# Image 0's tanh, tokens and features woven into its first layer, chunk by chunk

## The chip, the cores and the metric

The kernel runs on one core of one Trainium2 chip. The metric is the device time of one execution in microseconds (us), from the first to the last instruction of the core with a little around it. The engines are named as the profile names them: PE (TensorE, matrix products), DVE (VectorE), ACT (ScalarE), POOL (GpSimd) and SP (SyncE, which here issues the DMAs).

## What is computed

Eight images of 128 channels and 36x36 positions (1296 tokens) go through two layers. The first normalises in groups, convolves to queries, keys and values, and attends with a softmax; the second treats each position as a token, with an additive attention and a layer of 64 experts. Cut to what matters here:

```python
# layer 0, of the group-normalised x
x = conv1x1(inp, w_x)
q, k, v = conv3x3(x, w_qx), conv3x3_valid(x, w_kx), conv3x3_valid(x, w_vx)
a_x = softmax(q.T @ k) @ v                 # 1296 queries, 34*34 = 1156 keys
h = tanh(w_h[x, a_x, c-part] + b_h)
x = inp + w_o @ h + b_o
# layer 1, on tokens t (1296 x 128 per image)
n = layernorm(t)
s[i, j] = sum_d w[d] * tanh((n Wq)[i, d] + (n Wk)[j, d])   # additive scores
t = t + softmax(s) @ n
t = t + experts(layernorm(t))
```

## The kernel before, in words

The scores of layer 1 take nearly all of the time. The kernel writes the sum of tanh terms as quotients of products of exponentials over 8 blocks of 128 features (`NF = 8`). For one block of queries and one tile of keys a *slot* has four small products on PE, two denominators `d` and two numerators `n` (line 976), Ln and Exp of the denominators on ACT (999 and 1002: the reciprocal), the products of numerators and reciprocals on DVE (1027, 1029, 1033), and sums on POOL (1042). Twelve slots make a unit: one image, one chunk of 432 queries (`CH`, three chunks an image) and one tile of 128 keys (`KT`, eleven tiles, the last with 16 keys; `order` is 0, 1, 2, 3, 4, 10, 5, 6, 7, 8, 9).

All engines run in the order in which the code issues instructions; nothing is reordered. The order around the slots is written out with generators. A function such as `layer0`, `tokens` or `keys` issues a few instructions and yields: `matmuls(n)` asks for a turn on PE after n slots, `step(n)` for a turn without PE, `TAKE` to go on at once. During the slots four lanes hold such generators (`first_of_all`, `urgent`, `gates`, `background`). Every third slot gives a matmul turn; an allowance of 370 columns a slot (`PACE`) limits what a turn issues, except for `first_of_all`. The next image's first layer, tokens and keys run this way in `background` behind the current image's slots. Image 0 has no slots before it, so its preparation runs alone, at the start:

1. `normal(0)` normalises; `signs` lets POOL write a table of signs; `conv_keys(0)` convolves the keys.
2. `layer0(0)` (line 417) convolves the values, projects them (`vw`), and then for each chunk of 432 queries convolves the queries, makes scores and exponentials of ten key tiles, sums them, divides, and writes the chunk's part of `hpre` (line 506). The sums `tot` are made by POOL. Beside it, from its tenth step on, one step each of `context` (a constant part of the bias) and `features` (line 541: the weight products with `sign`, `a_q`, `a_k` and a few columns) is issued for each of its steps. After the third chunk one Tanh over all 1296 columns (line 509), which needs another table of functions than Exp and Ln, and three products with `w_o` whose results are added to x (line 517).
3. `tokens(0)` (line 589) transposes all eleven tiles, writes the tokens to memory (`tokd`), takes mean and variance of each token, raises the variance to the power -1/2 on POOL (line 265), transposes again and normalises into `xh`, and transposes that into `xT`.
4. `keys(0)` for the first tile, and four query blocks (`new_block`, lines 710 and 711), are issued in full; then the first three slots' denominators, and keys of two more tiles. Then the slots start, and the lane `urgent` holds the other keys.

In the slots, `exps` (line 1056) takes the exponential of a unit's scores. At the second one of each chunk it runs `urgent` until nothing is left in it.

`prefetch(u + 2)` loads the keys of the unit after next at the first slot of each unit, so a tile's keys have to be issued by then. Big tiles have eight buffers, chunk tiles (128x432) eight, and PSUM gives four banks to `aux` and the numerators.

Of the kernel before, what the change touches and what calls it, by code (L numbers as in the profile page):

```python
# [3 lines left out]

# [6 lines left out]
F32 = mybir.dt.float32  # L11
AF = mybir.ActivationFunctionType
ALU = mybir.AluOpType
# [59 lines left out]
def kernel(  # L73
# [56 lines left out]
    with ExitStack() as loop, ExitStack() as score:  # L130
# [143 lines left out]
        def step(rest=1):  # L274
            return (False, rest)

        def matmuls(rest=0):
            return (True, rest)
# [3 lines left out]
        def bmm(out, lhsT, rhs, **kw):  # L282
            behind[0] += max(out.free_size(), 128) + 20
            mm(out, lhsT, rhs, **kw)  # L284
# [123 lines left out]
        def conv_keys(b):  # L408
# [3 lines left out]
            for r0, nr in KROWS:  # L412
                yield from conv_turns(
                    taps["k"], (r0, nr), 1, grid(k[:, r0 * WV : (r0 + nr) * WV], WV), True
                )

        def layer0(b):

            r = xs[b][:, :N]
# [31 lines left out]
            for c in range(NCH):  # L451
# [52 lines left out]
                   xpad[:, 1 + c * RC : 1 + (c + 1) * RC, 1 : 1 + W], start=True, stop=True)  # L504
                yield TAKE
                nc.vector.tensor_add(hp[:, cols], px[:, :CH], ax)
                yield matmuls()
            yield step(2)
            nc.scalar.activation(hp, hp, AF.Tanh, bias=hb)
            nc.scalar.preload_act_table_set(LNEXP)  # L510
# [78 lines left out]
        def tokens(b):  # L589
# [74 lines left out]
                nc.sync.dma_start(xr[32 * i : 32 * i + REM], xh[:REM, NKT - 1, :])  # L664
            prepared[b] = (xh, xT, xr)

        def keys(b, tiles):

            xT = prepared[b][1]
            yield matmuls(1)  # L670
            for t in tiles:
# [4 lines left out]
                for q0 in (0, NF // 2):  # L676
                    some = slice(q0, q0 + NF // 2)
                    pk = aux("pk1").rearrange("p (q t) -> p q t", t=128)
                    for q in range(NF // 2):
                        bmm(pk[:, q, :n], a_k[:, (q0 + q) * 128 : (q0 + q + 1) * 128],  # L680
                           xT[:, o : o + n], start=True, stop=True)
                    yield TAKE
                    if first:
# [19 lines left out]
        def query_block(b, c, q, qf):  # L703

            xT = prepared[b][1]
            pq = aux("pq1")
            bmm(pq[:, :CH], a_q[:, q * 128 : (q + 1) * 128], xT[:, c * CH : (c + 1) * CH],
               start=True, stop=True)
            yield TAKE
            nc.scalar.activation(qf[:, 0, :], pq[:, :CH], AF.Exp, bias=fb_s[:, q : q + 1])  # L710
            nc.gpsimd.tensor_scalar(  # L711
                qf[:, 1, :], qf[:, 0, :], cs_s[:, q : q + 1], None, ALU.mult
            )
            yield matmuls()

# [210 lines left out]
        def drain(*gens):  # L926
            for g in gens:
                for _ in g:
                    pass
# [34 lines left out]
        def new_block(b, c, q):  # L964
            qf = qfp.tile([128, 2, CH], F32, tag="qf", name="qf")
            qf_of[b, c, q] = qf
            return query_block(b, c, q, qf)
# [88 lines left out]
        def exps(p, u, d):  # L1056
            b, c, j = units[u]

            while urgent and len(es.get((b, c), ())) == 1:
                urgent.run(p)  # L1060
            e = etp.tile([128, CH], F32, tag="e", name="e")
            nc.scalar.activation(e[:, : d.shape[-1]], d, AF.Exp, bias=eb_s)  # L1062
            es.setdefault((b, c), {})[j] = e
            if (b, c) == (NB - 1, NCH - 1) and len(es[b, c]) == NKT - 2:
                urgent.append(attend_early(b, c, es[b, c]))
            if len(es[b, c]) == NKT:
                urgent.append(attend(b, c, es.pop((b, c))))
# [61 lines left out]
        sign = signs()  # L1129
        drain(conv_keys(0))  # L1130

        aside = chain(context(), features(sign))
        for i, _ in enumerate(layer0(0)):
            if i > 8:
                next(aside, None)
        drain(aside)
        a_q, a_k, cs_s, fb_s, eb_s = (feat[n] for n in ("a_q", "a_k", "cs_s", "fb_s", "eb_s"))
        drain(tokens(0), keys(0, order[:1]))
        for i, q in enumerate(IN_TURN):
            if i < 4:  # L1140
                drain(new_block(0, 0, q))
            else:
                first_of_all.append(new_block(0, 0, q))
        for p in range(LAG):
            denominators(p)
        drain(keys(0, order[1:3]))
        prefetch(1)
        urgent.append(keys(0, order[3:]))
        pending = deque()
        for p, (u, k) in enumerate(slots):  # L1150
            b, c, j = units[u]
# [260 lines left out]
```

## Time and profile before

| | |
|---|---|
| median of 3 runs | 6119.27 us (6111.72 to 6121.77) |
| the profiled execution | 6131.19 us |
| its span, first to last instruction | 6129.5 us |
| PE / DVE / ACT / POOL busy | 92% / 78% / 87% / 75% of the span |
| last add into `hpre` of image 0 (line 506) | starts at 129.16 us |
| first denominator product of a slot | starts at 155.57 us |
| first numerator product of a slot | starts at 162.32 us |
| mean granted clock of TensorE | 0.982 of full speed |

The profile is one execution. A *stretch* view gives the busy time of each engine between two times, with the granted clock of PE as a share of full speed. The *timeline* gives instructions in order of time; in brackets it says how long the engine had been idle and what released it. The *chain of waits* goes back from the end, at each step to what released it. Matrix products in 32-bit floats show as two instructions each.

### The profile page before, as it was taken

What the parts mean: (1) busy time and instruction counts of PE and PEld (TensorE: products, weight loads), DVE (VectorE), ACT (ScalarE), POOL (GpSimd) and SP (SyncE); (2) the same over time, 40 slices, a digit from 0 to 9 for tenths busy, and PEclk for the clock granted to TensorE, in tenths of its full rate; (3) what the DMA queues carried; (4) which work ended last, traced back from release to release, by engine and by line L of the source; (5) the groups of instructions that cost most, each with busy time, mean ns of one, the idle gap of its engine ahead of it and who ended that gap; (6) DMA issues with size and microseconds to landing.
All of it is one profiled execution on the core that took longest, in us unless ns stands there. A gap on an engine that the chain in (4) does not pass through costs nothing.

```text
span 6129.5 us, 94280 instructions
## 1 busy us (share of the span) xinstructions
PE 5669.4 (92%) x33500; PEld 2928.9 (48%) x33500; DVE 4786.5 (78%) x9544; ACT 5338.2 (87%) x5859; POOL 4603.0 (75%) x2824
## 2 busy tenths in 40 slices
PE   7999999999999999999999999999999999988886
PEld 5554455544554445544445444454445544544433
DVE  4787878878788788877787777887778878788883
ACT  1999898998989989889998999899998998999991
POOL 4777777877778867778687786877777777777871
PEclk9999999999999999999999999999999999999998
DMA  1210021001110011100111001110011000110008
GB/s 44 73 34 22 25 74 40 20 25 33 66 39 20 26 46 54 37 24 23 61 39 39 22 24 65 40 33 23 28 62 49 24 25 28 66 50 29 28 20 286
DMA packets 150409, 270.42 MB, mean 44 GB/s; under 512 B 45553, under 2 KB 75633, under 8 KB 149937
## 3 DMA queue, kind: packets, MB, share of 16 engines
q1 hardware_dynamic: 149936, 264.39, 13.0%
q8 instruction: 264, 4.33, 0.3%
q14 instruction: 209, 1.70, 0.1%
HBM read 200.15 MB, written 63.93 MB: 43 GB/s over the span
## 4 chain that ended last, share of the span: by engine, by line
PE 54%; DVE 16%; ACT 15%; issue 11%; POOL 2%; DMA 1%; SPq 0%; DVEq 0%; POOLq 0%; ACTq 0%
PE d L976 18%; PE n L976 12%; ACT lq L999 11%; PE pa L284 7%; DVE rp L1033 7%; PE pc L284 5%; DVE n L1027 5%; PE s L284 3%; DVE accd L1029 2%; PE pq L284 2%; PE pk L284 1%; PE d L981 1%; PE n L981 1%; ACT e L1062 1%; DMA w<-in_weight_dram 1%
## 5 line engine op out<-in xcount | busy, mean ns | idle before, releaser
L1042 POOL TENSOR_TENSOR accp<-accp,rp 128x864 f32<-128x864 f32 x1439 | 2912.2, 2024 | 995.3 <-DVE rp L1033 951.4
L976 PE MATMUL d<-qf,kf 32*128 32x432 f32 (+1 forms) x11520 | 2785.5, 562 | 269.3 <-ACT lq L999 264.0
L976 PE MATMUL n<-qf,kf 32*128 32x432 f32 (+1 forms) x11520 | 2997.9, 556 | 31.0 <-DVE rp L1033 12.4
L999 ACT ACTIVATE lq<-d 128x864 f32<-128x864 f32 x2928 | 2483.2, 877 | 473.9 <-PE n L976 284.6
L1033 DVE TENSOR_TENSOR rp<-n,lq 128x432 f32<-128x432 f32 x3912 | 2180.2, 600 | 757.5 <-PE n L976 606.3
L1002 ACT ACTIVATE lq<-lq 128x864 f32<-128x864 f32 (+1 forms) x1944 | 2495.8, 1284 | 61.7
L976 PEld LDWEIGHTS d<-qf,kf 32*128 32x128 f32 (+1 forms) x11520 | 1024.4, 185 | 1447.4 <-ACT lq L999 1105.5
L976 PEld LDWEIGHTS n<-qf,kf 32*128 32x128 f32 (+1 forms) x11520 | 1263.1, 186 | 700.4 <-issue 294.8
L1029 DVE TENSOR_TENSOR accd<-n,accd 128x432 f32<-128x432 f32 x1440 | 866.1, 601 | 24.6
L1027 DVE TENSOR_TENSOR n<-n,lq 128x432 f32<-128x432 f32 x1440 | 810.3, 607 | 59.1 <-PE n L976 37.1
L1040 POOL TENSOR_TENSOR accp<-rp 128x864 f32<-128x864 f32 x240 | 485.6, 2023 | 286.6 <-DVE rp L1033 284.4
L284 PE MATMUL pa<-xh,e 128*108 128x129 f32 x1920 | 254.9, 281 | 32.7 <-DVE accd L1029 27.7
L284 PEld LDWEIGHTS pa<-xh,e 128*108 128x108 f32 x1920 | 221.0, 174 | 127.4 <-DVE accd L1029 102.6
L1051 POOL TENSOR_TENSOR accd<-accp,accd 128x432 f32<-128x432 f32 x239 | 265.4, 1110 | 18.7
L1049 POOL TENSOR_TENSOR accp<-accp 128x432 f32<-128x432 f32 x239 | 263.9, 1104 | 11.8
L711 POOL TENSOR_SCALAR qf<-qf,cs_s 128x432 f32<-128x432 f32 x192 | 260.3, 1366 | 9.2 <-ACT qf L710 9.2
L462 POOL TENSOR_TENSOR tot<-tot,e 116x432 f32<-116x432 f32 x192 | 212.2, 1105 | 9.0 <-ACT e L471 4.5
L284 PE MATMUL s<-q,k 128*116 128x432 f32 x480 | 207.0, 547 | 7.8 <-DVE accd L1029 5.5
L471 ACT ACTIVATE e<-s 116x432 f32<-116x432 f32 x240 | 116.3, 521 | 99.1 <-PE s L284 97.9
L284 PE MATMUL pa<-e,vw 116*128 116x432 f32 x480 | 196.8, 532 | 0.4
L284 PEld LDWEIGHTS pk<-xT,a_k 128*128 128x128 f32 x1408 | 164.8, 192 | 54.2 <-DVE accd L1029 43.5
L1022 DVE TENSOR_TENSOR accd<-n,lq 128x432 f32<-128x432 f32 x240 | 143.8, 599 | 49.6 <-ACT lq L1002 26.3
(223 smaller groups left out, 3826.5 us busy)
## 6 DMA issues: line engine op xcount, KB each, us to landing
kf<-kd SPq DMA_DIRECT2D x239, 512.0 KB
kd<-ks SPq DMA_DIRECT2D x158, 256.0 KB
w<-in_weight_dram SPq DMA_DIRECT2D x32, 1024.0 KB
wk_t<-wk_t_d SPq DMA_DIRECT2D x7, 768.0 KB
wv_t<-wv_t_d SPq DMA_DIRECT2D x7, 768.0 KB
wq_t<-wq_t_d SPq DMA_DIRECT2D x7, 768.0 KB
x<-in_x_dram SPq DMA_DIRECT2D x8, 648.0 KB
t<-tokd SPq DMA_DIRECT2D x96, 54.0 KB
```

What stands on the lines that cost most here:

```text
L284: mm(out, lhsT, rhs, **kw)
L711: nc.gpsimd.tensor_scalar(qf[:, 1, :], qf[:, 0, :], cs_s[:, q : q + 1], None, ALU.mult)
L976: mm(outs[h][:, :CH], kf[rows[h], q, :], qf_of[b, c, q][rows[h], part, :], start=True, stop=True)
L999: nc.scalar.activation(lq[:, o : o + n, :], d[:, :n, :CH], AF.Ln)
L1002: nc.scalar.activation(some, some, AF.Exp, scale=-1.0)
L1027: mult(ns[h], ns[h], lq[:, o + h, :])
L1029: nc.vector.tensor_add(live["d"], ns[h], live["d"])
L1033: mult(rp[:, h, :], n, lq[:, o + h, :])
L1040: nc.gpsimd.tensor_add(live["p"], live["r"], rp)
L1042: ending(u if k == NP - 1 else 0).tensor_add(live["p"], live["p"], rp)
L1049: ending(u).tensor_add(s[:, 0, :], s[:, 0, :], s[:, 1, :])
L1051: ending(u).tensor_add(d, s[:, 0, :], d)
```

## The change

In image 0 the tanh is no longer one Tanh over three chunks but is made for each chunk with a clamp, Exp, Ln and Exp (1 - 2/(1 + e^2x)), which are all in the table that the kernel uses anyway. `layer0(0)` returns after the last chunk of `hpre`. What followed, for image 0 alone, is a new generator `first_tokens(c, hp)` for each chunk: the tanh in four steps, the product with `w_o`, the sum with x, transposes, token statistics, normalisation and transposes for the tiles that the chunk completes (tiles 0 to 2, 3 to 5, 6 to 10). It transposes the tokens once, not twice, before it normalises.

The steps beside `layer0(0)` start later (after its step 24 instead of 8), and they are now a queue: `context`, `features`, then, when a chunk is done, its `first_tokens`; after chunk 1 also the keys of tile 0 and four query blocks. A step that asks for a rest makes the queue wait for twice as many steps of `layer0`. What is left at the end is issued at once, beside the third chunk's tanh. The rest of `first_tokens(2)` goes into the lane `urgent`, behind the keys of two tiles and ahead of the other keys, and `exps` doesn't empty the lane for the first chunk of image 0.

```diff
+        def tanh_parts(h):
+            def limited():
+                nc.vector.tensor_scalar(h, h, hb, 15.0, ALU.add, ALU.min)
+            def exp():
+                nc.scalar.activation(h, h, AF.Exp, scale=2.0)
+            def log():
+                nc.scalar.activation(h, h, AF.Ln, bias=ones[:, 0:1])
+            def share():
+                nc.scalar.activation(h, h, AF.Exp, scale=-1.0)
+                nc.gpsimd.tensor_scalar(h, h, -2.0, 1.0, ALU.mult, ALU.add)
+            return limited, exp, log, share
...
                 nc.vector.tensor_add(hp[:, cols], px[:, :CH], ax)
+                if b == 0:
+                    first_chunk_done(c, hp)
                 yield matmuls()
+            if b == 0:
+                return
             yield step(2)
...
+        def first_tokens(c, hp):
+            r = xs[0][:, :N]
+            if c == 0:
+                xh = big_tile("xh")[:, : NKT * (C + 1)].rearrange("p (t c) -> p t c", c=C + 1)
+                nc.gpsimd.memset(xh[:, :, C : C + 1], 1.0)
+                xr = two.tile([128, C + 1], F32, tag="xr", name="xr")
+                prepared[0] = (xh, big_tile("xT")[:, :N], xr)
+            xh, xT, xr = prepared[0]
+            cols = slice(c * CH, (c + 1) * CH)
+            for part in tanh_parts(hp[:, cols]):
+                yield step(1)
+                part()
+            yield matmuls(2)
+            po = aux("po0")
+            bmm(po[:, :CH], wo_s, hp[:, cols], start=True, stop=True)
+            yield TAKE
+            nc.vector.scalar_tensor_tensor(
+                r[:, cols], po[:, :CH], bo_s, r[:, cols], ALU.add, ALU.add
+            )
+            yield matmuls(1)
+            for some in ([(0, 1, 2)], [(3, 4, 5)], [(6, 7, 8), (9, 10)])[c]:
+                tp = aux("tpl")
+                for i, t in enumerate(some):
+                    o, n = KT[t]
+                    turned_to(tp[:n, i * C : (i + 1) * C], r[:, o : o + n], ident)
+                yield TAKE
+                tok = chunk_tile("tok")[:, : 3 * C].rearrange("p (t c) -> p t c", c=C)
...
+                nc.vector.tensor_copy(
+                    tok[:, :full, :], tp[:, : full * C].rearrange("p (t c) -> p t c", c=C)
+                )
+                o = KT[some[0]][0]
+                nc.sync.dma_start(
+                    tokd[0][o : o + full * 128].rearrange("(t p) c -> p t c", p=128),
+                    tok[:, :full, :],
+                )
...
+                for i, t in enumerate(some):
+                    n = KT[t][1]
+                    nc.vector.bn_stats(st[:n, i, :], tok[:n, i, :])
+                    nc.vector.bn_aggr(mv[:n, i, :], st[:n, i, :])
+                ve = plus_eps(mv[:, : len(some), 1], 1e-5, [128, len(some)])
+                yield step(1)
+                rs = small.tile([128, 3], F32, tag="ln_rs", name="ln_rs")[:, : len(some)]
+                rsqrt(rs, ve)
+                yield step(2)
+                for i, t in enumerate(some):
+                    n = KT[t][1]
+                    nc.vector.tensor_scalar(
+                        xh[:n, t, :C], tok[:n, i, :], mv[:n, i, 0:1], rs[:n, i : i + 1],
+                        ALU.subtract, ALU.mult,
+                    )
+                yield matmuls(1)
+                tp = aux("tpc")
+                for i, t in enumerate(some):
+                    n = KT[t][1]
+                    turned_to(tp[:, i * 128 : i * 128 + n], xh[:n, t, :C], ident[:n, :n])
+                yield TAKE
+                lo, hi = KT[some[0]][0], KT[some[-1]][0] + KT[some[-1]][1]
+                nc.vector.tensor_copy(xT[:, lo:hi], tp[:, : hi - lo])
+                yield matmuls()
...
-            while urgent and len(es.get((b, c), ())) == 1:
+            while urgent and (b, c) != (0, 0) and len(es.get((b, c), ())) == 1:
                 urgent.run(p)
...
-        aside = chain(context(), features(sign))
+        aside = deque([context(), features(sign)])
+
+        def first_chunk_done(c, hp):
+            if c == NCH - 1:
+                urgent.append(first_tokens(c, hp))
+                return
+            aside.append(first_tokens(c, hp))
+            if c == 1:
+                aside.append(keys(0, order[:1]))
+                aside.extend(new_block(0, 0, q) for q in IN_TURN[:4])
+
+        rest = 0
         for i, _ in enumerate(layer0(0)):
-            if i > 8:
-                next(aside, None)
-        drain(aside)
...
-        drain(tokens(0), keys(0, order[:1]))
-        for i, q in enumerate(IN_TURN):
-            if i < 4:
-                drain(new_block(0, 0, q))
-            else:
-                first_of_all.append(new_block(0, 0, q))
+            if rest > 0 or i <= 24 or not aside:
+                rest -= 1
+                continue
+            says = next(aside[0], 0)
+            if says == 0:
+                aside.popleft()
+            elif says is not None:
+                rest = 2 * says[1]
+        left = list(aside)
+        for i in range(5):
+            next(urgent[0])
+            drain(*left[i : i + 1])
+        drain(*left[5:])
+        first_of_all.extend(new_block(0, 0, q) for q in IN_TURN[4:])
         for p in range(LAG):
             denominators(p)
         drain(keys(0, order[1:3]))
         prefetch(1)
-        urgent.append(keys(0, order[3:]))
+        urgent.appendleft(keys(0, order[3:5]))
+        urgent.append(keys(0, order[5:]))
```

## The prediction

> **What bounds the kernel now.** I read the page first: how full each engine is over the whole span.
>
> ```profile
> PE 5669.4 (92%) x33500; PEld 2928.9 (48%) x33500; DVE 4786.5 (78%) x9544; ACT 5338.2 (87%) x5859; POOL 4603.0 (75%) x2824
> ```
>
> The change touches image 0 only, so the average says little. I then asked for the busy time of each engine in stretches: 30 to 66 us (the values' convolution, the features, the first query convolution), 66 to 129 (the three chunks of image 0's attention), 129 to 162 (from the last chunk to the first slot), and in the slots 196 to 230 (with keys) and 230 to 262 (without).
>
> ```profile
> core 0: us, PE busy (x) PEld busy (x) DVE busy (x) ACT busy (x) POOL busy (x), PEclk, DMA share, GB/s
> 30.00:66.00 36.00, 30.29 (x166) 26.59 (x164) 13.80 (x43) 0.00 (x0) 17.02 (x19) 0.91 0.01 1
> 66.00:129.00 63.00, 58.24 (x180) 32.71 (x180) 16.54 (x33) 20.50 (x37) 29.75 (x28) 1.00 0.00 0
> 129.00:162.00 33.00, 21.81 (x106) 14.75 (x107) 13.79 (x46) 11.66 (x14) 7.61 (x6) 0.79 0.12 38
> 196.00:230.00 34.00, 33.21 (x216) 18.93 (x214) 25.55 (x47) 33.65 (x40) 23.56 (x14) 1.00 0.38 130
> 230.00:262.00 32.00, 25.13 (x152) 12.08 (x154) 30.34 (x58) 31.59 (x34) 25.70 (x17) 1.00 0.10 30
> ```
>
> In 66 to 129 PE is the bound and DVE, ACT and POOL are mostly idle. In 129 to 162 nothing is full: a chain. In the slots ACT is full (31.59 of 32 us), DVE follows (30.34), PE has a fifth to spare without keys. The chain of waits, 112 to 166 us, gives the serial stretch (start, length, engine, work):
>
> ```profile
> 129.16 0.62 DVE hpre L506
> ...
> 129.80 1.38 ACT hpre L509
> ...
> 131.23 4.15 PE po L284 x6
> ...
> 136.07 1.55 DVE tok L608 x3
> ...
> 142.83 2.16 POOL ln_rs L265
> ...
> 147.07 2.61 PE tpc L288 x11
> 149.68 3.06 PE pk L284 x16
> 152.74 2.90 PE pq L284 x8
> 155.64 0.95 PE d L976 x8
> ```
>
> From the last `hpre` to the first `d` 26 us go by, one engine at a time. The timeline of PE has another hole earlier, and the start of the slots' numerators (start, length; in brackets the idle time before and its releaser):
>
> ```profile
> 47.62 2.07 PE L556 MATMUL pa<-sign,wT 128*128 128x512 f32 x2 [5.69 <-POOL sign L532]
> ...
> 66.46 3.16 PE L284 MATMUL s<-q,k 128*116 128x432 f32 x8 [0.48 <-DVE q L316]
> ...
> 162.32 0.60 PE L976 MATMUL n<-qf,kf 32*128 32x432 f32 x1
> ```
>
> The features' matmul waits for the signs that POOL writes until 47.56, with the values' convolution queued behind it on PE.
>
> **What the Trainium skill says.** "ScalarE: Activation LUTs", section "What ACT_TABLE_LOAD costs", gives a load of 1283 ns, and its section "Table sets: the hidden batching unit" says that one set holds Exp and Ln. The trace agrees: loads of 1.28 us stand only around the Tanh (127.42 and 131.19), none between Ln and Exp. "TensorE: Matmul & The Clock Gate", section "What's actually happening", says that PE goes to half clock after an idle window of some 3.4 us. The trace agrees: granted clock 0.51 in 48 to 53 us, just after the wait for the signs, and 0.50 in 145 to 149, in the serial stretch. "Trainium Architecture — The Big Picture", section "Inside one NeuronCore", says that each engine runs its own stream and meets the others only at semaphores: a step woven into another engine's idle time is free, but its wait holds whatever is queued behind it. The hole at 47 us is one.
>
> **The change, part by part.** All sums are against the profiled execution (span 6129.5, its time 6131.19). The unprofiled runs have the median 6119.27, 12 us less; I take the difference over to it unchanged.
>
> (a) *Features later.* The steps beside image 0's layer started at step 9; now they start at step 25, when the values' convolution is issued (steps 1 to 24). The signs are then long done and PE meets no hole. PE's work from 29.9: convolution of v 12 groups, 4 at 1.13 and 8 at 1.04 (the cadence of the keys' convolution just before) = 12.8; projection vw 2.4; context 2.06 + 0.28; two transposes 0.3 each; four sign products of 2 x 0.43, with overheads 3.6; the query convolution 4.5; the products for `cs` 1.9, which now cover the 0.8 us that the first scores waited for q. Sum 28.2 with 1 us of hand-offs 29.2: first scores at 59.1 instead of 66.46. Gain 7.4: the hole of 5.7 and the half clock behind it. The DMA of `wvc_s` has only its place among the steps moved; SP has nothing else queued there.
>
> (b) *Chunk 0's and chunk 1's tokens inside chunks 1 and 2.* Added to each of them: on PE the output product 0.72, three transposes twice, 0.45 + 0.5: 1.7 us, which bounds there, so it counts in full. On DVE the clamp 0.4 (128x384 took 0.36), residual 0.67, and copies, statistics and normalisation 4.1, beside 8 us busy of 22. ACT takes Exp, Ln, Exp of 0.55 each. POOL takes the share 1.37 (the row of `qf`, same shape) and the power over 3 columns, about 1.0 (11 took 2.15, one 0.60 to 0.83); it has 0.65 us to spare per two score tiles, and the chunk's end waits for its total already (PE `pt` 0.92). I take 1.0 more for that and for PE standing at `po`, where the share may be 0.3 late. Cost 2.7 a chunk, 5.4 in all; bounds 3.4 (PE alone) and 12. Their SP writes to `tokd` land under the chunk. The clamp, two Exps and Ln have no row of their own before; same-shape rows stand in. Chunk buffers: `tok` takes one of eight for about 4 us; q, tot and ax hold three, four stay for e, and an e lives about 3.5 us with a new one each 0.7 to 2 us. Just enough; taken as nothing.
>
> (c) *The serial stretch.* Gone: Tanh with its load, the long chain of tokens. First keys (`pk`, x16) and four query blocks stay; the keys now stand around chunk 2's `pt`, at full clock about 2.05 as in the slots. From the start of `pt` (125.24): pt 1, pk 1, pa 1.45, pk 1, px and pq0 1.4: first query Exp on ACT at 131.3. Then ACT is the path: four query Exps 2.8 and, between them, chunk 2's Exp, Ln, Exp 1.7: denominators' Ln at 135.6; Ln and Exp of three slots 5.0: 140.6; the first keys of the next tile 0.6, which free the PSUM buffer of the first numerator: 141.2. Before it was 162.3. Gain 21.1.
>
> (d) *Chunk 2's tokens in the slots.* After four key turns the lane gives `po` at slot 11, then transposes, statistics and normalisation up to about slot 26. ACT takes nothing of it, PE 2.5 us that its spare fifth hides. DVE is what it costs: residual 0.67; first group of three tiles 0.55 + 1.19 + 0.17 + 0.98 + 0.55; second 0.27 + 0.27 + 0.78 + 0.17 + 0.65 + 0.30, memset 0.1: 6.65. Its slack is 0.37 per three slots of 4.97 (4.6 busy), 1.9 over five turns, with half a key more 2.4: 4.3 stick out. POOL's two powers, 1.8, add 0.7. Cost 5; bounds 0 (the DVE work of image 1's normalisation at 247 to 255 stretched nothing) and 12. Keys behind it move from slots 8 to 29 to slots 8 to 47, each at least a unit ahead of its load; image 1's own steps start no later than the lane's rests allow, and they now end at 849 us with 53 us to spare before image 1.
>
> (e) *No emptying at the second exponential of (0,0).* Before, the lane was empty by then (last keys at 223.3, that exponential at 226.25): nothing. It only keeps (d) from a burst.
>
> Sum: -7.4 + 5.4 - 21.1 + 5.0 = -18.1, so 6111.4 for the profiled time's span and **6101** for the median.
>
> **Rivals.** *Less of it arrives* (6111): in-order waits inside chunks 1 and 2 cost 12 instead of 5.4, and the slots 8 instead of 5: -7.4 + 12 - 21.1 + 8 = -8.5 remain. For it: POOL has little slack there, and every step stands on two engines. Against: each step is put three to six steps after what it needs, 1.4 us or more. *The slots absorb everything* (6094): (d) costs nothing and (b) PE alone, -7.4 + 3.4 - 21.1 = -25.1. For it: image 1's normalisation passed unseen. Against: DVE's slack is counted. *Slower* (6137): the tokens' steps starve the slots until PE's clock halves. In image 1's slots, 755 to 765, it fell to 0.66 right after the tokens' statistics, and ACT was busy 5.91 of 10 us. That is some 4 us a time. Five such drops (20 us) eat the gain of the forecast, eight make it slower by over 12 us, nine give 6101 + 36; so many need the late keys to keep the lanes stumbling into image 1. Against: in early slots PE was busy 3.17 of 5 us (250 to 255) at full clock. *The weaving is not real* (6119): the steps run in order behind the chunks; against: the loop issues them by count.
>
> **Chances.** Forecast 0.60, absorbed 0.14, less of it 0.17, no effect 0.03, slower 0.06. The forecast's own range, 6096 to 6107, comes from the bounds of (b) and (d) met halfway. The 8-in-10 range reaches to both neighbours: 6092 to 6113. About 0.2% (12 us) is what a measurement of this kernel can tell. The forecast's cases lie nearly all below 6107: 0.60 and 0.14, plus little of the third, make 0.75 faster; 0.19 same; 0.06 slower.
>
> **What would show it.** (a): no PE idle before the sign product, first scores near 59. (b): chunks of 22.3 us grow to about 25, PE's wait before `pt` below 2 us. (c): no table load near 127 to 131; from `pt` to the first numerator 16 us, not 37. (d): ACT idle between slots 11 and 26 in all 5 us, granted clock 1. Wrong it would be with chunks near 30 us, a clock below 0.9 in the first 60 slots, or image 1's first slot less than 10 us earlier than before.

## The result and the profile after

The changed kernel takes 6096.94 us, median of 7 runs (6091.02 to 6103.35). The kernel before takes 6116.33 in 7 runs (6111.72 to 6131.01; the three behind the prediction are among them). The ratio is 0.9963, with an interval of 0.9954 to 0.9973: 19.4 us faster, 0.37%, where 18.1 were predicted.

The profiled execution after has a span of 6095.2 us at a granted clock of 0.986; the one before had 6129.5 at 0.982. These two differ by 34 us, more than the medians, but at the last of the landmarks below they are only 19.6 us apart and stay so to the end of image 0; the rest comes up in images 1 to 7, whose code is the same. So I read the early part of the traces and leave the totals to the medians.

Four places in time serve as landmarks in every trace: the first scores; the sum over the exponentials of chunk 2 (`pt`, the end of chunk 2's scores); the first numerator product of the slots; and the fifth exponential of a unit's scores in time, some 62 slots later. (This one belongs to the short tile of 16 keys, whose unit has two slots, not twelve; the scores of the tile ahead of it come just after.)

| landmark, us | before | after | difference | predicted |
|---|---|---|---|---|
| first scores start | 66.46 | 57.36 | -9.1 | -7.4 (a) |
| scores to `pt` of chunk 2 (three chunks) | 58.78 | 62.78 | +4.0 | +5.4 (b) |
| `pt` to first numerator | 37.08 | 15.14 | -21.9 | -21.1 (c) |
| first numerator to fifth exponential | 121.64 | 129.11 | +7.5 | +5.0 (d) |
| sum, at the fifth exponential | 283.96 | 264.39 | -19.6 | -18.1 |

How full the engines are over the whole span has hardly moved, from the first section of the page after:

```profile
PE 5656.7 (93%) x33489; PEld 2916.0 (48%) x33489; DVE 4792.3 (79%) x9553; ACT 5338.6 (88%) x5865; POOL 4606.6 (76%) x2829
```

There are 9 instructions more on DVE, 6 on ACT and 5 on POOL and 11 fewer on PE, and the busy times of all five differ by less than 13 us from before. The gain is in when they are busy. The stretches of the kernel after, for the features (30 to 59 us), the three chunks (59 to 122), from chunk 2's end to the first numerator (122 to 135), and two pieces of the first 32 slots (busy us of PE, weight loads, DVE, ACT and POOL with instruction counts, then granted clock, DMA share and GB/s):

```profile
core 0: us, PE busy (x) PEld busy (x) DVE busy (x) ACT busy (x) POOL busy (x), PEclk, DMA share, GB/s
30.00:59.00 29.00, 28.98 (x172) 25.78 (x171) 14.41 (x45) 0.53 (x1) 17.32 (x19) 1.00 0.01 2
59.00:122.00 63.00, 58.71 (x196) 33.84 (x195) 28.54 (x58) 21.41 (x41) 32.48 (x32) 1.00 0.02 7
122.00:135.00 13.00, 11.43 (x66) 7.40 (x65) 2.28 (x4) 10.35 (x16) 5.93 (x5) 1.00 0.11 42
165.00:190.00 25.00, 23.65 (x114) 11.87 (x114) 24.50 (x61) 22.54 (x23) 17.85 (x12) 1.00 0.30 96
195.00:200.00 5.00, 4.98 (x32) 4.39 (x36) 1.64 (x3) 1.46 (x4) 3.81 (x5) 0.68 0.02 5
```

Before, 30 to 66 us had PE busy 30.29 of 36 us at a clock of 0.91; now it is busy 28.98 of 29 at 1.00. In the chunks DVE went from 16.54 to 28.54 us, in idle time. In 122 to 135 ACT is busy 10.35 of 13 us, where the old stretch of 33 us had it busy 11.66. Then come two places that are not so good: in 165 to 190 DVE is full (24.50 of 25) and ACT, the engine that sets the pace of the slots, stands 2.5 us; in 195 to 200 the clock is 0.68 and ACT stands 3.5 of 5 us. The chain of waits at the end of chunk 2, from the kernel after (start, length, engine, work), runs as step (c) laid it out:

```profile
120.14 0.99 PE pt L283 x2
121.14 0.89 PE pk L283 x8
...
125.11 1.46 PE pq L283 x4
...
126.59 0.62 ACT qf L804
127.22 0.45 ACT hpre L422
...
129.23 0.45 ACT hpre L428
129.68 0.79 ACT lq L1093
...
133.01 1.64 ACT lq L1096
```

The tanh's exponentials and logarithm (`hpre`, 0.45 us each) stand between the query exponentials (`qf`), and the denominators follow at once. No table is loaded. The features and the first numerator, from the timeline after:

```profile
48.66 1.88 PE L576 MATMUL pa<-sign,wT 128*128 128x512 f32 x4
57.36 0.96 PE L283 MATMUL s<-q,k 128*116 128x432 f32 x2
135.28 0.60 PE L1070 MATMUL n<-qf,kf 32*128 32x432 f32 x1
```

The sign product has no bracket: PE didn't stand before it (5.69 us before the change).

Of the signs of being wrong that the prediction named, one came: a clock below 0.9 in the first 60 slots (0.68 in 195 to 200 us). It lasted for a few us; over 135 to 264 us the clock is 0.99. The experiments take it up.

### The profile page after: what moved, and what is told of

Read it like the earlier page. It is cut to its first block, busy times and chain, and to the rows that moved or that the text cites. A ratio compares the mean times of both kernels' runs of the same rounds, so it can differ in the third digit from the quotient of the medians.

```text
span 6095.2 us, 94288 instructions
## 1 busy us (share of the span) xinstructions
PE 5656.7 (93%) x33489; PEld 2916.0 (48%) x33489; DVE 4792.3 (79%) x9553; ACT 5338.6 (88%) x5865; POOL 4606.6 (76%) x2829
## 3 DMA queue, kind: packets, MB, share of 16 engines
q1 hardware_dynamic: 149984, 264.39, 13.1%
## 4 chain that ended last, share of the span: by engine, by line
PE 55%; DVE 17%; ACT 15%; issue 11%; POOL 2%; DMA 1%; DVEq 0%; ACTq 0%; POOLq 0%
PE d L1070 18%; PE n L1070 12%; ACT lq L1093 11%; PE pa L283 7%; DVE rp L1127 7%; DVE n L1121 5%; PE pc L283 5%; PE s L283 3%; DVE accd L1123 2%; PE pq L283 2%; PE pk L283 1%; PE d L1075 1%; PE n L1075 1%; ACT e L1156 1%; ACT ks L781 1%
```

## The experiments

I had three questions. Do the parts (a), (c) and (d) cost and bring what the sum says, each alone? Why do the slots lose 7.5 us: is it the DVE work of chunk 2's tokens, as (d) says, or something that meets it there? And what holds the chunks longer than PE's own work? Every kernel computes the whole result. All ratios are to the kernel before, on the same chip, with 95% intervals; a and n stand for the first scores and the first numerator, and the last column is from there to the fifth exponential.

| kernel | median us | ratio | a | n | slots |
|---|---|---|---|---|---|
| again (the kernel after) | 6098.15 | 0.9956 (0.9943 to 0.9968) | 57.24 | 135.15 | 129.67 |
| a_only | 6114.35 | 0.9985 (0.9977 to 0.9993) | 58.56 | 155.68 | 121.58 |
| no_a | 6106.64 | 0.9973 (0.9963 to 0.9983) | 68.17 | 145.85 | 129.51 |
| c2_serial | 6106.74 | 0.9969 (0.9957 to 0.9982) | 57.15 | 154.46 | 120.86 |
| bg_late | 6089.38 | 0.9948 (0.9935 to 0.9960) | 57.26 | 135.19 | 122.12 |
| emptied | 6104.98 | 0.9970 (0.9959 to 0.9980) | 57.04 | 134.99 | 137.53 |
| tanh_table | 6111.00 | 0.9979 (0.9970 to 0.9989) | 56.94 | 142.35 | 128.12 |
| twice | 6101.87 | 0.9965 (0.9951 to 0.9978) | 58.60 | 135.38 | 129.20 |
| bg_unit2 | 6095.29 | 0.9962 (0.9948 to 0.9976) | 57.14 | 136.74 | 123.43 |
| dev_pool | 6091.06 | 0.9957 (0.9944 to 0.9969) | 57.12 | 136.74 | 125.82 |
| bg_late_twice | 6094.21 | 0.9960 (0.9947 to 0.9972) | 57.12 | 133.90 | 122.40 |
| bg_late_again | 6086.41 | 0.9945 (0.9932 to 0.9958) | 58.83 | 136.73 | 122.06 |

The kernels from again to c2_serial shared one chip, those from bg_late to twice another, bg_unit2 to bg_late_twice a third.

### The kernel after once more

> The changed kernel once more. In the first profile the loss inside the slots, 7.5 us between the first numerator (135.3 us) and the fifth exponential of a unit's scores (264.4 us; 162.3 and 284.0 before), stood partly at a drop of PE's clock to one half at 197 to 200 us. Theory A (the drop follows from the order of the work): it comes back in this execution, and the fifth exponential stands at 264.4 again, within 1 us. Rival (the drop was this one execution's): the clock stays at 1.00 and the fifth exponential comes 3 to 4 us earlier.

No edit. The ratio is 0.9956 beside 0.9963, and the landmarks are within 0.6 us of the first profile. The drop of the clock is there again (0.62 in 195 to 200 us), so the loss in the slots belongs to the kernel and not to one execution.

### Features later, alone and undone

In the kernel before:

```diff
-            if i > 8:
+            if i > 24:
```

> The kernel before with one edit: context and features start after step 24 of image 0's layer, not after step 8. Theory: the wait for the signs and the half clock behind it are a cause of their own; first scores at 57.4 instead of 66.5 us, first numerator 9 us earlier (153.2), the whole 9 us shorter (ratio 0.9985). Rival: without the other parts the features' work only moves the wait into the query convolution; first numerator less than 4 us earlier.

And in the kernel after:

```diff
-            if rest > 0 or i <= 24 or not aside:
+            if rest > 0 or i <= 8 or not aside:
```

> The changed kernel with the features put back to start after step 8. Theory: first scores back at 66.5 us, all that follows as in the changed kernel but 9 us later: first numerator 144.4, fifth exponential of a unit's scores 273.5, the whole 9 us longer than the changed kernel. Rival (parts interact): the later start moves the tokens' steps against the chunks or the slots, and the fifth exponential stands off 273.5 by over 2 us.

Undone, the first numerator comes 10.6 us later (145.85 against 135.28), with the first scores at 68.17, and the fifth exponential stands at 275.36, 1.9 from what was expected. The first scores stood at 66.46 before; the 1.7 more are a second half clock, 0.57 in 60 to 64 us of this execution. Alone, the first scores come at 58.56 instead of 66.46, 7.9 earlier, but at the first numerator 6.6 us are left. The stretches of a_only (columns as above) show where the rest went:

```profile
56.00:60.00 4.00, 3.32 (x21) 2.62 (x22) 0.94 (x6) 0.38 (x1) 0.00 (x0) 0.99 0.00 0
60.00:64.00 4.00, 4.00 (x8) 1.84 (x7) 0.00 (x0) 1.74 (x4) 2.20 (x3) 0.58 0.00 0
```

PE stood 0.68 us in 56 to 60, after the products for `cs` that have two columns each, and then ran at a clock of 0.58: 1.7 us gone in chunk 0. The median moved by 7.4 us between before and a_only, which is what step (a) said, and the ratio is the 0.9985 expected. The same drop of the clock, at 44 to 52 or 55 to 65 us, came in twice, bg_unit2, dev_pool and bg_late_again, whose code up to there is that of the kernel after; there it cost 1.2 to 1.7 us. Whether it comes differs between executions.

### Chunk 2's tokens not in the slots

```diff
         drain(*left[5:])
+        drain(urgent.popleft())
```

> The changed kernel, but what is left of chunk 2's tokens is issued in full before the first slot, so that nothing but keys is left for the lane. Theory: the loss of 7.5 us in the slots comes from these tokens; it vanishes, and their serial length of some 11 us (residual 0.7, then twice transposes, statistics, power, normalisation, transposes: 6 and 4.5) comes ahead of the first numerator: that at 146, the fifth exponential at 268, 3.5 later than in the changed kernel. Rival: the loss comes from the keys' later place or from image 1's earlier start; then it stays and the fifth exponential stands at 275.

The rest of `first_tokens(2)` runs alone before the slots, as all tokens did before. The slots then take 120.86 us to the fifth exponential, as before the change (121.64) and 8.3 less than after; but the first numerator comes at 154.46, 19.2 later. At the fifth exponential (d) is thus worth 10.9 us, in the median 8.6 (6106.74 against 6098.15 on the same chip). I had expected some 11 for the serial steps, not 19.2; the fifth exponential falls on the rival's 275 (275.32), but with the loss in the slots gone, not with the loss kept. The stretch of c2_serial shows where the time is:

```profile
135.00:150.00 15.00, 7.61 (x28) 3.90 (x29) 5.52 (x23) 3.80 (x5) 1.58 (x2) 0.50 0.07 20
```

PE is busy half of the time, and its clock is at half for the whole of it, as it was in 145 to 149 us before.

### Image 1's first steps later

```diff
+                if c == 0 and j == (4 if b == 0 else 1):
                     if b + 1 < NB:
                         background.extend(
```

> The changed kernel, but image 1's own steps (its normalisation first) go into the background lane at unit 4 of image 0, not at unit 1, so they no longer fall between the steps of chunk 2's tokens. Theory: the half clock at 197 to 200 us comes from both together (a step of image 1's normalisation stood 1.94 us on DVE while POOL summed, PE had little to do, and the next keys ran at half clock); it vanishes, and the fifth exponential of a unit's scores comes 3 to 4 us earlier than 264.4. Rival: the tokens' DVE work alone costs the 7.5 us; the fifth exponential stays within 1 us of 264.4.

The generators of image 1, its normalisation first, start at unit 4 and not at unit 1. The slots take 122.12 us instead of 129.11, with all of chunk 2's tokens still in them: 7.0 us, where 3 to 4 were expected. Not all of it is the meeting of two works. The times from one exponential of scores to the next show where each kernel differs (the first from the first numerator, all in us; bg_unit2 and dev_pool are runs further down):

| kernel | to 1st | to 2nd | to 3rd | to 4th | to 5th | to 6th | to 7th |
|---|---|---|---|---|---|---|---|
| before | 40.09 | 23.83 | 20.42 | 20.42 | 16.86 | 8.67 | 27.64 |
| after | 38.39 | 28.63 | 24.32 | 20.91 | 16.86 | 8.67 | 27.64 |
| c2_serial | 39.33 | 23.83 | 20.42 | 20.42 | 16.86 | 8.67 | 27.65 |
| bg_late | 38.39 | 23.31 | 24.33 | 20.91 | 15.17 | 6.23 | 24.62 |
| bg_unit2 | 38.37 | 23.30 | 24.31 | 20.90 | 16.56 | 6.10 | 28.88 |
| dev_pool | 38.37 | 25.40 | 24.30 | 20.90 | 16.86 | 8.67 | 27.64 |
| emptied | 38.38 | 35.96 | 20.44 | 22.80 | 19.95 | 6.39 | 28.01 |

The tokens and image 1's normalisation meet on the way to the second exponential, and there bg_late is 5.3 us shorter than after. Up to the fourth, after is 7.5 us longer than before, bg_late 2.2 longer and c2_serial 0.8 shorter. So image 1's steps without the tokens take no more than they did before the change, chunk 2's tokens without image 1's steps cost 2.2 us, and both together cost 5.3 more. The 2.2 are not the tokens' own work: up to the second exponential, which covers it, bg_late is even 2.2 us ahead of before. It falls back by 4.4 on the way to the third and fourth, where the keys now lie that the tokens push back: emptied, which has made these keys by then, takes 20.44 us to the third, as before did.

The 1.7 us that bg_late gains on the way to the fifth, and more to the sixth and seventh, don't come from the tokens, which are through by then. There the kernels before and after make image 1's next steps (its products `px` and `pc`, at 248 to 298 us in after), which bg_late makes later; before and after have the same times there. A late start of image 1 should then gain in the kernel before too; no run tried that. Two stretches of bg_late, to put beside those of after:

```profile
165.00:190.00 25.00, 24.23 (x122) 12.21 (x123) 24.44 (x59) 23.74 (x25) 19.46 (x13) 1.00 0.12 38
...
195.00:200.00 5.00, 4.59 (x40) 2.74 (x33) 4.30 (x8) 4.80 (x6) 3.87 (x6) 1.00 0.33 84
```

ACT stands 1.3 us instead of 2.5 in the first, 0.2 instead of 3.5 in the second, and the clock is whole. DVE is as full in the first stretch as in after (24.44 against 24.50 us), so a full DVE alone is not the loss. The median is 6089.38, the lowest up to here.

### The short step between two sums

What happens at 190 to 200 us in the kernel after can be read from its timeline (in brackets the idle time before and its releaser):

```profile
190.36 2.01 POOL L1134 TENSOR_TENSOR accp<-rp 128x864 f32<-128x864 f32 x1
190.46 1.94 DVE L361 SCALAR_TENSOR_TENSOR dev<-dev,gn_mv 128x1 f32<-128x1 f32 x1
...
192.97 1.50 PE L1070 MATMUL n<-qf,kf 64*128 64x432 f32 x4 [0.49 <-DVE rp L1127]
...
195.02 3.89 PE L283 MATMUL pk<-xT,a_k 128*128 128x16 f32 x24 [0.55 <-DVE accd L1123]
```

`dev` is a step of image 1's normalisation: one column, 1.94 us. It starts 0.1 us after POOL's sum and ends with it. The Trainium skill, "SBUF — State Buffer", section "SBUF: two separate sides", says that DVE and POOL share a pair of ports to SBUF as an exclusive lock, also for a DVE step with two inputs from SBUF beside a POOL step that reads SBUF, and that the later one "fully blocks". The 1.94 beside the 2.01 agree; in image 0's own normalisation at 8 us, with no sum of the slots on POOL yet, the same step takes 0.22. DVE's products for the slots wait behind it, PE has less to do (busy 3.98 of 5 us in 190 to 195), its clock falls, and the next key turn, 24 products of 16 columns, takes 3.89 us. For image 1, I gave the steps to POOL:

```diff
-            nc.vector.tensor_sub(dev, mv[:, 0:1], gm)
-            nc.vector.scalar_tensor_tensor(dev, dev, dev, mv[:, 1:2], ALU.mult, ALU.add)
+            if b == 1:
+                nc.gpsimd.tensor_sub(dev, mv[:, 0:1], gm)
+                nc.gpsimd.tensor_mul(dev, dev, dev)
+                nc.gpsimd.tensor_add(dev, dev, mv[:, 1:2])
+            else:
+                nc.vector.tensor_sub(dev, mv[:, 0:1], gm)
+                nc.vector.scalar_tensor_tensor(dev, dev, dev, mv[:, 1:2], ALU.mult, ALU.add)
```

> The changed kernel with the three small steps on the group means of image 1 (128x1) on POOL instead of DVE. On DVE one of them stood 1.94 us at 190.5 us while POOL summed, the products behind it waited, and 4 us later the clock was at one half. Theory: that one wait brings the drop; the clock stays at 1.00 and the fifth exponential comes 3 to 4 us before 264.4. Rival: the slots are loose all through 175 to 195 us and the clock falls all the same; fifth exponential within 1 us of 264.4.

The timeline of dev_pool has three steps of a fifth of a microsecond in place of it:

```profile
193.78 0.18 POOL L361 TENSOR_TENSOR dev<-gn_mv,gm 128x1 f32<-128x1 f32 x1
194.04 0.19 POOL L362 TENSOR_TENSOR dev<-dev 128x1 f32<-128x1 f32 x1
194.32 0.19 POOL L363 TENSOR_TENSOR dev<-dev,gn_mv 128x1 f32<-128x1 f32 x1
```

And the stretch in which the clock had fallen has it whole, with ACT busy 3.87 instead of 1.46 us:

```profile
195.00:200.00 5.00, 4.76 (x42) 3.69 (x44) 2.59 (x6) 3.87 (x7) 4.91 (x6) 1.00 0.01 3
```

The slots take 125.82 us: 3.3 of the 7.5 were this one step and the clock behind it. (The fifth exponential comes only 1.8 us earlier than after, where 3 to 4 were expected, since this execution stood 1.5 us later at the first numerator, by the early drop of the clock.) In the median the 3.3 us do not show: 0.9957 beside 0.9956 and 0.9963. Another 2.1 us of the meeting stay, which bg_late does not have; how they divide among single waits isn't shown.

The step alone is harmless. In the kernel before it was held up just as long, with nothing of the tokens around it:

```profile
248.95 2.02 POOL L1042 TENSOR_TENSOR accp<-accp,rp 128x864 f32<-128x864 f32 x1 [0.84 <-DVE gm L359]
249.10 1.88 DVE L362 SCALAR_TENSOR_TENSOR dev<-dev,gn_mv 128x1 f32<-128x1 f32 x1
```

ACT was busy 4.94 of the 5 us in 250 to 255, the clock stayed at 1.00, and the exponentials around it are 20.42 us apart, as without it. In c2_serial and bg_unit2 it took 1.89 us and cost nothing that can be seen. All six profiles that have both works in these slots (after, again, no_a, emptied, tanh_table, twice) show one of the two steps on `dev` blocked for 1.8 to 1.9 us and the fall of the clock behind it. So the half clock takes the block and the tokens together. Little work for PE is not enough as a reason: in the kernel before PE was busy only 3.17 of 5 us there. What brings the clock down in one case and not in the other stays open.

### Image 1's first steps at unit 2

Against bg_late:

```diff
-                if c == 0 and j == (4 if b == 0 else 1):
+                if c == 0 and j == (2 if b == 0 else 1):
```

> The changed kernel with image 1's own steps put into the background lane at unit 2 (slot 24), between unit 1 (changed kernel: fifth exponential of a unit's scores at 264.4 us, half clock near 197) and unit 4 (257.3, no half clock). Theory: it is the tokens (slots 11 to 26) and image 1's normalisation in the same slots that cost; from slot 24 on they hardly meet, the clock stays at 1.00 and the fifth exponential stands at 257 to 260. Rival: image 1's normalisation costs as much beside the keys that come back at slot 29; fifth exponential at 263 or later.

One unit later than in the kernel after is enough to end the meeting: up to the fourth exponential bg_unit2 is level with bg_late. By then most of chunk 2's tokens are through. At the fifth the slots have taken 123.43 us, 5.7 less than after. At the first numerator this execution is 1.5 us late by the early drop of the clock, and the fifth exponential stands at 260.17. In the median (0.9962) this gain does not show either.

### The lane emptied at once

```diff
-            while urgent and (b, c) != (0, 0) and len(es.get((b, c), ())) == 1:
+            while urgent and len(es.get((b, c), ())) == 1:
```

> The changed kernel with the lane emptied at once again at the second exponential of image 0's first chunk. The tokens are done by then, but some four and a half tiles of keys are left: 9 us of PE at once, of which ACT uses 5. Theory: the exception is worth these 4 to 5 us; fifth exponential at 269. Rival: nothing is lost, as these keys have to be made anyway; fifth exponential within 1 us of 264.4.

This undoes (e) alone. The lane of keys is then run out in one go at the second exponential. The timeline and the stretch behind it, in emptied:

```profile
199.57 8.84 PE L283 MATMUL pk<-xT,a_k 128*128 128x128 f32 x72
```

```profile
205.00:210.00 5.00, 5.00 (x43) 4.03 (x43) 0.58 (x2) 3.55 (x7) 0.00 (x0) 1.00 0.74 272
```

PE makes keys for 8.84 us, POOL has nothing to do, and ACT is busy 3.55 of 5 us. The slots take 137.53 us, 8.4 more than after (8.1 at the fifth exponential, where 4 to 5 were expected). At the end of image 0 some 3 to 5 us of this are left, and the median is 6104.98, a ratio of 0.9970 whose interval overlaps those of the kernel after. So the edit that step (e) costed at nothing against before saves 8 us at this place against the change without it, and less, or too little to settle, in the whole.

### The tanh from its own table

```diff
-            for part in tanh_parts(hp[:, cols]):
+            for part in range(4):
                 yield step(1)
-                part()
+                if part == 3:
+                    nc.scalar.activation(hp[:, cols], hp[:, cols], AF.Tanh, bias=hb)
+                    nc.scalar.preload_act_table_set(LNEXP)
```

> The changed kernel with the table's Tanh in place of clamp, Exp, Ln, Exp and share, still chunk by chunk (two loads of 1.28 us each time). Theory: in the chunks the loads stand between the exponentials of scores and PE waits, about 2 us each; at the end ACT is the path, 3.1 us in place of 1.8; first numerator at 140 to 141, fifth exponential 5 to 6 us later than 264.4. Rival: ACT's idle time hides the loads in the chunks; first numerator at 136.6, fifth exponential 1 to 2 us later.

Everything stays woven, but each chunk's tanh is one Tanh with its table loads. ACT in chunk 1, from the timeline of tanh_table:

```profile
81.06 1.28 ACT L700 ACT_TABLE_LOAD   x1
82.36 0.65 ACT L700 ACTIVATE hpre<-hpre,hb 128x432 f32<-128x432 f32 x1
83.03 1.28 ACT L701 ACT_TABLE_LOAD   x1
```

For 3.2 us ACT makes no exponential of the scores. Chunk 1 takes 25.94 instead of 24.16 us, and the first numerator comes 7.1 later (142.35, beyond the 140 to 141 expected). The median is 6111.0, and the gain over the kernel before is 0.21% where the change has 0.37%. The weaving works with either tanh; the rewriting, which needs no other table, is worth these 7 us.

### The tokens turned twice

After the power, in `first_tokens`:

```diff
-                yield step(2)
+                yield matmuls(2)
+                tp = aux("tpn")
+                for i, t in enumerate(some):
+                    o, n = KT[t]
+                    turned_to(tp[:n, i * C : (i + 1) * C], r[:, o : o + n], ident)
+                yield TAKE
...
-                        xh[:n, t, :C], tok[:n, i, :], mv[:n, i, 0:1], rs[:n, i : i + 1],
-                        ALU.subtract, ALU.mult,
+                        xh[:n, t, :C], tp[:n, i * C : (i + 1) * C], mv[:n, i, 0:1],
+                        rs[:n, i : i + 1], ALU.subtract, ALU.mult,
```

> The changed kernel, but the normalisation reads the tokens from PSUM after a second transposition (as the kernel before did), not from the copy in SBUF. In the changed kernel three normalisations stood 3.47 us on DVE, as long as POOL summed beside them, and an exponential waited for the chunk buffer that they held. Theory: a DVE step with its operands in SBUF waits for POOL's; from PSUM it takes 0.35 us each, chunks 1 and 2 are 0.5 to 1 us shorter in spite of 0.5 us more PE. Rival: PE is the bound all the same, and chunks 1 and 2 are 0.5 us longer each.

The reason is in the timeline of the kernel after, in chunk 1:

```profile
89.38 3.45 POOL L478 TENSOR_TENSOR tot<-tot,e 116x432 f32<-116x432 f32 x3
89.44 3.47 DVE L743 TENSOR_SCALAR xh<-tok,ln_mv,ln_rs 128x128 f32<-128x128 f32 x3 [0.37 <-POOL ln_rs L264]
92.96 0.33 PE L287 MATMUL tpc<-ident,xh 128*128 128x128 f32 x1 [0.69 <-DVE xh L743]
92.99 0.53 ACT L487 ACTIVATE e<-s 116x432 f32<-116x432 f32 x1 [2.49 <-DVE xh L743]
```

Three normalisations take 3.47 us beside POOL's three sums (3.45), PE stands 0.69 for the third, and an exponential waits 2.49 for a chunk buffer that they hold. When POOL is idle, three take 0.86 (c2_serial, 139.00). Read from PSUM in place of SBUF they are hardly held up by POOL's sums, in twice:

```profile
90.62 3.46 POOL L478 TENSOR_TENSOR tot<-tot,e 116x432 f32<-116x432 f32 x3
...
93.13 1.04 DVE L748 TENSOR_SCALAR xh<-tpn,ln_mv,ln_rs 128x128 f32<-128x128 f32 x3
```

Chunks 1 and 2 become 0.57 us shorter each (23.59 and 23.59 against 24.16 and 24.16), in spite of three transposes more in each. So the block costs a bit over 1 us in the two chunks, net of the transposes. The early drop of the clock hid it in this execution's landmarks, and in the median (6101.87, 0.9965) it is too small to see. In the slots, the other small step on `dev` is the one that is held up here (1.81 us beside a sum of 2.03), and the clock falls to 0.69 in 195 to 200 us all the same.

### The two edits together, and the better one again

> Both edits that gained so far: image 1's steps from unit 4 of image 0 on, and the normalisation from PSUM after a second transposition. Theory: they act in different stretches and add up; chunks 1 and 2 together 1.1 us shorter than with the late start alone, fifth exponential at 256.2 (1.2 later if the first projections fall into a half clock as they did in one run), the whole 1 us shorter than with the late start alone, too little to tell in the time. Rival: the second transpositions cost PE in the slots and eat the 1.1; fifth exponential at 257.3 or later.

> The version with image 1's steps from unit 4 on once more, to tell whether it is faster than the changed kernel (ratios so far 0.9948, interval 0.9935 to 0.9960, against 0.9963 and 0.9956). Theory: the 7 us saved in image 0's slots stay in the whole; ratio 0.9948 again, below 0.9955. Rival: what image 0 saves is lost where image 1's steps end later; ratio 0.9956 or above. In the trace the fifth exponential of a unit's scores stands at 257.3, the half clock is absent in either case.

bg_late_twice is bg_late and twice in one; its fifth exponential comes at 256.30 us, 8.1 earlier than after (264.39), which is what the two give when added. But its median is 6094.21, 0.9960, not below bg_late. The time doesn't confirm the microsecond that the early trace shows. bg_late again, on another chip: 6086.41, 0.9945 (0.9932 to 0.9958), with slots of 122.06 us as in its first profile. Its fifth exponential stands at 258.79, later than the 257.3 expected by the early drop of the clock. It is the best of these kernels and faster than before by 0.5% in both its measurements. It shared no chip with the kernel after, whose interval (0.9954 to 0.9973) overlaps its own, so its lead over the change, 5 to 11 us by the ratios, is likely rather than settled; the traces have 7 us of it at the fifth exponential.

## Why the prediction was right

The forecast of 6101 us (6092 to 6113) met 6096.94, and the gain of 18.1 us met 19.4, by the mechanism that it named: work that stood alone goes into idle time, and a hole of PE and a serial chain are gone. That the sum is so close is in part luck: (a), (b) and (c) gave some 4 us more than they were priced at, and (d) cost 2.5 more. By its steps:

(a) *Features later.* Right, a little small: 9.1 us instead of 7.4. The hole and the half clock are gone; the sum of PE's work from the start of the values' convolution was 29.2 us and measured 27.0. The 1 us for hand-offs in it did not come (PE was busy 28.98 of 29 us), and the pieces themselves took about 1 us less than the rows they were priced by. a_only and no_a give this part 7.4 and 8.5 us of the median.

(b) *Tokens inside chunks 1 and 2.* Right in kind, mis-sized in its terms: 3.8 us for the two chunks, not 5.4 (chunk 0 grew by 0.2). The 1.0 us a chunk that it added to PE's 1.7 was too much; each chunk grew by 1.9. PE's work doesn't count in full either: in twice, which has 0.5 us more of it by the same prices, each grew by only 1.3. The term for POOL's share was 1.37 us, from a row of the same shape, and it took 0.555: that row multiplies by a column per partition, the share uses constants. These two groups of POOL's instructions in the kernel after (count, sum, mean ns, idle before) have the same shapes:

```profile
L429 POOL TENSOR_SCALAR hpre<-hpre 128x432 f32<-128x432 f32 x3 | 1.7, 555 | 20.4 <-ACT hpre L428 20.4
L805 POOL TENSOR_SCALAR qf<-qf,cs_s 128x432 f32<-128x432 f32 x192 | 260.4, 1366 | 6.5 <-ACT qf L804 6.5
```

The term that was missing is the block between DVE and POOL, 0.57 us a chunk by twice. The prediction had the engines meet only at semaphores and took a step in another engine's idle time as free; here POOL's sums held DVE up inside a step, not at a wait for a semaphore. "Just enough; taken as nothing" for the chunk buffers was not quite so, by the wait of 2.49 us above, which is part of the same delay. PE's wait before `pt` is 0.52 us, below the 2 that were named.

(c) *The serial stretch.* Right: 15.1 us from `pt` to the first numerator where 16 were said, ACT as the path, no table load. (Its sub-sums are off by up to 0.2 us: 131.3 and 4.5 make 135.8, not 135.6.) c2_serial and tanh_table show two of its causes one by one: the tokens in line cost 19.2 us there, the tables 7.1 over the three chunks and the stretch.

(d) *Chunk 2's tokens in the slots.* This is the step that failed in its cause, though its bounds of 0 to 12 held the 7.5. It said that 6.65 us of DVE work less a slack of 2.4 stick out, for 5 us with POOL's part. Without image 1's steps they don't: the tokens cost 2.2 us (bg_late, to the fourth exponential), and these fall where the keys now lie that the step moved back and priced at nothing. Its own sign, ACT idle for 5 us between slots 11 and 26, was 2.7 us (158 to 194), at full clock. The other 5.3 us come from image 1's normalisation in the same slots, which the step allowed for only as "steps start no later than the lane's rests allow". 3.3 of them are one blocked step of one column and the half clock behind it; how the other 2 divide among single waits isn't shown. So the 5 came near the 7.5 by two errors, a price too high for the tokens and none for the meeting.

(e) *No emptying.* The words hold ("only keeps (d) from a burst"); emptied gives the burst a size, about 8 us in the slots and 3 to 5 at the end of image 0.

The rivals. *Absorbed* missed the slots' 7.5; without image 1's steps 2.2 of them would be left. *Less of it arrives* is out in its first part, as the chunks grew by 4.0, not 12; its 8 us for the slots were nearer than the forecast's 5. *Slower* had the right kind of event, slots starved around a half clock, at about the price it gave (4 us; 3.3 by dev_pool), but it came once in the first 60 slots where eight were needed. *Not real* fell with the first profile.

Open: in the profiles bg_late is ahead of the kernel after by 7 us at the fifth exponential, 12.5 at the seventh, and 9 to 12 at the end of image 0 (its second profile has the smaller lead). What comes behind the fourth exponential goes with image 1's own steps, not with the tokens, and how much of it the kernel before would gain by a late start isn't known.

## What to carry to other kernels

Work woven into another stage's idle time is costed against everything else that is put into that stage: in these slots one stream cost 2.2 us alone and the other no more than before, both together cost 7.5, and putting one of them a unit later took 5.3 of it back. Compare two kernels step by step along the path, not at one landmark: a version that makes some work later can look better at a landmark that lies ahead of that work. Where DVE and POOL run side by side, look in the timeline for a small DVE step that lasts as long as POOL's instruction beside it; reading its input from PSUM (as in the run twice) or moving it to POOL (dev_pool) took the block away here. And take a duration from a row with the same kinds of operands, not only the same shape.

## What was unexpected of the hardware

- The block between DVE and POOL isn't listed as a wait but as busy time of the blocked step: 1.94 us for 128x1 (0.22 at 8 us, without the slots' sums on POOL), and 3.47 us for three normalisations of 128x128 that take 0.86 when POOL is idle and 1.04 from PSUM beside it.
- POOL's `tensor_scalar` on 128x432 took 0.555 us for a multiply and an add with two constants, and 1.366 for one multiply with a column per partition, also at 126.6 us, where DVE stood idle beside it.
- "Busy" PE doesn't always keep its clock, and a loosely filled one doesn't always lose it (3.17 of 5 us busy at 250 to 255 before, clock 1.00). After products of two columns (the `cs` products at 56 us) it fell to 0.58 in a_only with PE listed as busy 3.32 of 4 us ahead of it, and in the same code of the other kernels it fell in some executions and not in others.
